# Whitening on neighbouring partitions, and a third depthwise tap on TensorE, in a four-layer hybrid kernel

## The chip, the cores and the metric

The kernel runs on one core of a Trainium2 chip. The metric is the device time of one execution in microseconds. Before the change three runs gave 7655.76, 7665.0 and 7673.1 us; their median is 7665.0 us.

## The reference

The input is x, 8 images of 56 x 56 pixels with 128 channels, float32. Four layers follow one another; the change touches the first two.

Layer 0 is a deformable convolution block. From each image it computes a depthwise 3x3 convolution, a batch norm and a gelu; a matrix product of that with `w_off` and `w_msk` gives, per pixel, 4 groups x 9 points x (two offsets and one mask logit). The masks go through a softmax over the 9 points. The image, projected by `w_in`, is then sampled bilinearly at each point plus its offset, weighted by the masks and summed; a projection, two layer norms and a small two-layer network follow. All offsets of the given data have a magnitude of at most 1.

Layer 1 is a decorrelating batch norm ("whitening"). The flat activation is seen as 64 rows. In outline:

```
x1_s  = every ninth element of each of the 64 rows
mean1 = mean of x1_s per row
cov   = x1_s x1_s^T / n  + 0.01 I          (64 x 64; x1_s as it is)
D     = cov^(-1/2), by five Newton-Schulz steps
y     = D (x1 - mean1)
```

The kernel takes its sample in two halves of a row, with the same stride. Layers 2 and 3 are token layers with attention and a mixture of experts; they take most of the time.

## The kernel before

**Layer 0.** `conv_layer` first prepares all images, then samples. Preparation is a loop over n from -1 to 8 that calls, in this order, `hidden(n-1)`, `image(n+1)`, `first_taps(n+1)`, `other_taps(n)`, on odd n `projection` of the pair (n-1, n), and `offsets(n-1)`. A scheduler of the framework decides the order on each engine from this program order, the data dependences and the buffers.

- `image` (L266, L271): loads an image (`xs`), transposes it on PE into PSUM (`p_x`) and copies it with seven ACT copies into `xp`, a padded image; two images share one `xp` tile, and there are two such tiles. Seven more ACT operations (L276) make strided copies `xT`, which SP's queue stores.
- `first_taps` (L315, L322): the first `NTE` of the nine taps of the depthwise convolution as products with diagonal matrices (`taps`), summed in PSUM (`p_dw`), seven pieces of 448 columns per image; ACT copies each piece to `acc`. A float32 product is two instruction records.
- `other_taps` (L327): the other taps on DVE, one multiply-add of 128x3136 each.
- `hidden` (L341): gelu on ACT, seven pieces.
- `projection` (L288, L295): `w_in` on the padded pair, with a bias addition on DVE, and stores into `strips` in device memory.
- `offsets` (L356 to L370): products `p_om`, seven additions on DVE into `om`, then a maximum and a negated minimum over all offsets of the image (L365, L366), which land in two columns of `far`, then `mask_softmax` (L430 to L435: maximum, subtraction, Exp on ACT, sum, reciprocal, multiplication), then a store of `om`.

After the loop the largest of all values in `far` is found (L393 to L398) and compared: `near` is 1 where it is at most 1. All engines load `near` and branch. `sample_near` relies on offsets of magnitude at most 1 and multiplies with small dense matrices; `sample_any` gathers with indirect DMAs. Before the loop, `zero` is written by two DMAs into the first and last two rows of `strips`, and sixteen small ones follow on the same queue, that of ACT.

**Layer 1.** `whiten_layer` holds the whole activation in SBUF as `x`, 128 partitions of 25,088 columns (12.85 MB). Partition h x 64 + b holds half h of row b, so each DMA (3,584 columns) reads 64 rows of one half into 64 partitions, fourteen in all on SP's queue. For each half: a reduction of the strided sample (`tot`, L900), 22 transposes of the sample (L912, 64x64 each out), 22 copies (L921) and 22 products of the piece with itself, summed in `cov` (L922). `p_mean` (L934) adds the sums of the two halves. Then come `a` (covariance plus 0.01 I), its norm, and five Newton-Schulz steps that alternate small PE products and DVE copies (L968 to L978). `both` (L983 to L986) is a 128x128 matrix with D in two diagonal blocks. For each of seven column ranges DVE subtracts the mean in place (L989), PE multiplies by `both` in seven pieces (`p_o`, L995), DVE and ACT copy alternately to `o`, and two DMAs of 64 partitions store it (L1003). The next layer reads y from device memory.

Of the kernel before, what the change touches and what calls it, by code (L numbers as in the profile page):

```python
# [17 lines left out]
NB, IH, IW, C = 8, 56, 56, 128  # L18
S = IH * IW
T = 112  # L20
NT = S // T
# [6 lines left out]
GP = GRP * NP  # L28
# [3 lines left out]
VW = IW + 4  # L32
PH, PX, NX = 7, 4, 14
SW = PX + 4
# [1 line left out]
R4 = 4 * C  # L36

NPX = 6
NTE = 2


WB, WCOLS, WSTEP, WITER, WEPS = 64, NB * S * C // 64, 9, 5, 0.01
WHALF = WCOLS // 2
# [84 lines left out]
def conv_layer(tc, k, x, w, z):  # L128

    nc = tc.nc  # L130
    n_batch = x.shape[0]
    with ExitStack() as ctx:
        cp = ctx.enter_context(tc.tile_pool(name="l0c", bufs=1))
# [30 lines left out]
        with tc.tile_pool(name="l0m", bufs=1) as mp:  # L164
            mean = mp.tile([128, 4], F32, name="mean")
# [13 lines left out]
            for b, name in ((q.b_out, "b_out"), (q.b2, "b_fc2")):  # L179
                row = row_bc(nc, mp, w[name], 128, name + "_row")  # L180
# [15 lines left out]
        gam = row_bc(nc, cp, w["gamma2"], T, "gam2r")  # L196
        nc.vector.tensor_tensor(q.sft2, q.sft2, gam, ALU.mult)

        far = cp.tile([T, 2 * n_batch], F32, name="far")
        near = cp.tile([1, 1], I32, name="near")  # L200
        with ExitStack() as pre:
            ip = pre.enter_context(tc.tile_pool(name="l0i", bufs=1))
            hp = pre.enter_context(tc.tile_pool(name="l0h", bufs=2))
            ps = pre.enter_context(tc.tile_pool(name="l0p", bufs=8, space=PSUM))
# [28 lines left out]
            nc.vector.tensor_tensor(bn_t, bn_t, bn_s, ALU.mult)  # L233
            nc.vector.tensor_tensor(bn_t, bn_t, bn_b, ALU.add)

            zero = ip.tile([NX * n_batch, 2 * SW * C], F32, name="zero")
            nc.gpsimd.memset(zero, 0.0)
            rows = q.strips.rearrange("n k y s c -> (n k) y (s c)")
            for y in (0, VW - 2):
                nc.scalar.dma_start(  # L240
                    rows[:, y : y + 2].rearrange("k y s -> k (y s)"), zero
                )
            for n in range(n_batch):
                for at in (q.strips[n, 0, :, :2], q.strips[n, NX - 1, :, SW - 2 :]):
                    nc.scalar.dma_start(
# [104 lines left out]
            def offsets(n, hT):  # L350

                om = hp.tile([T, NT, 3 * GP], F32, name="om")
                for r in range(PH):
                    p = ps.tile([T, GT, 3 * GP], F32, tag="m", name="p_om")
                    for i in range(GT):
                        nc.tensor.matmul(  # L356
                            p[:, i, :],
                            hT[:, r, i].rearrange("p a b -> p (a b)"),
                            w_om,
                            start=True,  # L360
                            stop=True,
                        )
                    nc.vector.tensor_tensor(om[:, r * GT : (r + 1) * GT, :], p, b_om, ALU.add)
                off = om[:, :, : 2 * GP]
                nc.vector.tensor_reduce(far[:, 2 * n : 2 * n + 1], off, AX.XY, ALU.max)  # L365
                nc.vector.tensor_reduce(  # L366
                    far[:, 2 * n + 1 : 2 * n + 2], off, AX.XY, ALU.min, negate=True
                )
                mask_softmax(nc, hp, om)
                nc.sync.dma_start(q.om[n], om)  # L370


# [51 lines left out]
def mask_softmax(nc, pool, om):  # L424

    n_t = om.shape[1]
    m = om[:, :, 2 * GP :].rearrange("p t (q g) -> p t g q", g=GRP)
    msum = pool.tile([T, n_t, GRP], F32, name="msum")
    mb = msum.unsqueeze(3).to_broadcast([T, n_t, GRP, NP])
    nc.vector.tensor_reduce(msum, m, AX.X, ALU.max)  # L430
    nc.vector.tensor_tensor(m, m, mb, ALU.subtract)
    nc.scalar.activation(om[:, :, 2 * GP :], om[:, :, 2 * GP :], AF.Exp)
# [433 lines left out]

def whiten_layer(tc, k, z, y):

    nc = tc.nc
    n_half = -(-WCOLS // WSTEP) // 2  # L870
    first = (0, -WHALF % WSTEP)
    n_tr = -(-n_half // 128)
    WC = 7 * 512
    zf = z.rearrange("h n w c -> (h n w c)").rearrange("(r s) -> r s", r=WB)
    yf = y.rearrange("h n w c -> (h n w c)").rearrange("(r s) -> r s", r=WB)
    with ExitStack() as ctx:
        bp = ctx.enter_context(tc.tile_pool(name="l1b", bufs=1))
        wp = ctx.enter_context(tc.tile_pool(name="l1w", bufs=3))
# [2 lines left out]
        ps1 = ctx.enter_context(tc.tile_pool(name="l1p1", bufs=1, space=PSUM))  # L881
        ps2 = ctx.enter_context(tc.tile_pool(name="l1p2", bufs=2, space=PSUM))


        x = bp.tile([2 * WB, WHALF], F32, name="x")
        for c in range(0, WHALF, WC):
            for h in range(2):
                nc.sync.dma_start(
                    x[h * WB : (h + 1) * WB, c : c + WC],
                    zf[:, h * WHALF + c : h * WHALF + c + WC],  # L890
                )


        smp = bp.tile([128, 2 * n_tr * WB], F32, name="smp")
        cov = ps1.tile([WB, WB], F32, name="cov")
        tot = bp.tile([2 * WB, 1], F32, name="tot")
        n_mm = 0
        for h in range(2):
            rows = slice(h * WB, (h + 1) * WB)
            nc.vector.tensor_reduce(  # L900
                tot[rows],
                x[rows, first[h] : first[h] + WSTEP * (n_half - 1) + 1 : WSTEP],
                AX.X,
                ALU.add,
            )
            for i0 in range(0, n_tr, 8):
                p = ps.tile([128, 8, WB], F32, tag="m", name="p_smp")
                m = min(8, n_tr - i0)
                for i in range(i0, i0 + m):
                    n = min(128, n_half - i * 128)  # L910
                    a = first[h] + i * 128 * WSTEP
                    nc.tensor.transpose(  # L912
                        p[:n, i - i0, :],
                        x[rows, a : a + WSTEP * (n - 1) + 1 : WSTEP],
                        k.ident[rows, rows],
                    )
                for i in range(i0, i0 + m):
                    n = min(128, n_half - i * 128)
                    at = (h * n_tr + i) * WB
                    s = smp[:n, at : at + WB]  # L920
                    nc.vector.tensor_copy(s, p[:n, i - i0, :])  # L921
                    nc.tensor.matmul(  # L922
                        cov, s, s, start=(n_mm == 0), stop=(n_mm == 2 * n_tr - 1)
                    )
                    n_mm += 1

        n_smp = float(2 * n_half)
        fold = bp.tile([2 * WB, 2, WB], F32, name="fold")
        for h in range(2):
            nc.vector.tensor_tensor(  # L930
                fold[:, h], k.ident[:, :WB], k.ident[:, WB:], ALU.add
            )
        p = ps.tile([2 * WB, 1], F32, tag="m", name="p_mean")
        nc.tensor.matmul(  # L934
            p, fold.rearrange("p a b -> p (a b)"), tot, start=True, stop=True
        )
        mean = bp.tile([2 * WB, 1], F32, name="mean")
        nc.vector.tensor_scalar(mean, p, 1.0 / n_smp, None, ALU.mult)
# [4 lines left out]
        nc.vector.scalar_tensor_tensor(a, cov, 1.0 / n_smp, ieps, ALU.mult, ALU.add)  # L943


        sq = bp.tile([WB, WB], F32, name="sq")
# [19 lines left out]
        for _ in range(WITER):  # L966
# [12 lines left out]
        dm = bp.tile([WB, WB], F32, name="dm")  # L979
        nc.vector.tensor_scalar(dm, zm, rinv, None, ALU.mult)  # L980
        both = bp.tile([2 * WB, 2 * WB], F32, name="both")
        nc.vector.memset(both, 0.0)
        nc.vector.tensor_copy(both[:WB, :WB], dm)  # L983
        p = ps2.tile([2 * WB, WB], F32, tag="ns", name="p_low")
        nc.tensor.matmul(p[WB:], k.ident[:WB, :WB], dm, start=True, stop=True)
        nc.vector.tensor_copy(both[WB:, WB:], p[WB:])  # L986

        for c in range(0, WHALF, WC):
            nc.vector.tensor_scalar(  # L989
                x[:, c : c + WC], x[:, c : c + WC], mean, None, ALU.subtract  # L990
            )
            o = wp.tile([2 * WB, WC], F32, name="o")
            for i in range(0, WC, 512):
                p = ps.tile([2 * WB, 512], F32, tag="m", name="p_o")
                nc.tensor.matmul(  # L995
                    p, both, x[:, c + i : c + i + 512], start=True, stop=True
                )
# [4 lines left out]
            for h in range(2):  # L1002
                nc.sync.dma_start(  # L1003
                    yf[:, h * WHALF + c : h * WHALF + c + WC],
                    o[h * WB : (h + 1) * WB],
                )

# [1378 lines left out]
```

## Time and profile before

| | |
|---|---|
| median of three runs | 7665.0 us |
| profiled execution | 7657.94 us |
| its span | 7656.2 us |
| mean granted TensorE clock | 0.908 |
| layer 0: last multiplication of the preparation ends | 433.2 us |
| layer 0: sampling starts on DVE | 443.3 us |
| layer 1: first load of `x` issued | 1437.8 us |
| layer 1: last load of `x` lands | 1496.05 us |
| layer 1: `both` ready | 1531.9 us |
| layer 1: last stores of y issued | 1577.3 us |
| layer 2: first load of y issued | 1589.05 us |

Times inside the profile are counted from the start of the span. The profile's parts are: busy time of each engine (PE is TensorE, PEld its weight loads, DVE VectorE, ACT ScalarE, POOL GpSimd, SP the sync engine whose queue issues DMAs); the span in 40 slices; groups of instructions by line with the mean time of one and the idle time ahead of them; waits; and windows, which give each engine's busy time in a stretch. "L327" is a line of the kernel before. In a group, "out<-in" are the program's tile names, followed by the shapes and by the number of instructions.

### The profile page before, as it was taken

The page shows a single profiled execution, that of the slowest core. Times are in us where ns is not written, and L with a number is a line of the kernel's source. Part 1 is how long each engine was busy: PE and PEld are TensorE (multiplying, and loading weights), DVE is VectorE, ACT ScalarE, POOL GpSimd, SP SyncE. Part 2 cuts the span into 40 slices and gives each one's busy share as a digit, 9 for nine tenths or more (in the row PEclk, how much of TensorE's full clock was granted, in tenths as well). Part 3 has the DMA queues.
Part 4 walks back from the last instruction along what each step waited for, and adds up shares of the span by engine and source line. Part 5 has one row for each costly group of instructions (what it writes and reads, how often), then busy time and mean ns, then how long its engine had stood idle before and what let it go on. Part 6 is the DMA issues. An engine that isn't in the chain of part 4 may idle for free. (4 is left out here: it accounts for less than half of the span.)

```text
span 7656.2 us, 158331 instructions
## 1 busy us (share of the span) xinstructions
PE 6459.4 (84%) x59947; PEld 2867.8 (37%) x59947; DVE 5281.9 (69%) x9840; ACT 4163.3 (54%) x6499; POOL 2939.2 (38%) x2555
## 2 busy tenths in 40 slices
PE   6659999565899999999999999999999999556764
PEld 4446666333233333333333323323323323235542
DVE  7975564356677777777777777777777777356761
ACT  4424444122566666666666666666666666146750
POOL 0001111022344444444444444444444444333763
PEclk9768899776999999999999999999999999789877
DMA  5453343376787877778777778878778777544544
GB/s 156 135 121 78 85 97 65 83 227 215 191 207 191 197 188 192 197 190 195 197 191 192 197 187 197 198 188 196 195 191 197 190 185 181 198 111 113 137 134 142
DMA packets 737846, 1287.45 MB, mean 168 GB/s; under 512 B 119235, under 2 KB 504645, under 8 KB 730053
## 3 DMA queue, kind: packets, MB, share of 16 engines
q1 hardware_dynamic: 727092, 1260.77, 65.5%
q0 software_dynamic: 6144, 12.60, 0.5%
q8 instruction: 486, 7.96, 0.4%
q10 hardware_dynamic: 3824, 3.68, 0.2%
q14 instruction: 300, 2.45, 0.1%
HBM read 286.04 MB, written 197.81 MB: 63 GB/s over the span
## 5 line engine op out<-in xcount | busy, mean ns | idle before, releaser
L1260 ACT ACTIVATE e<-p_s 128x768 f32<-128x768 f32 (+2 forms) x3712 | 2887.8, 830 | 1588.2 <-PE p_s L1252 1320.1
L1298 POOL COPY x<-sq 32x1152 f32<-32x1152 f32 x1792 | 2062.2, 1151 | 2017.6 <-PE p_s L1252 1241.2
L1271 DVE STREAM_TRANSPOSE sq<-e 128x768 f32<-128x768 f32 x2688 | 2434.3, 950 | 516.0 <-ACT e L1260 258.9
L1252 PE MATMUL p_s<-q,kT 32*128 32x384 f32 (+2 forms) x14848 | 1892.8, 548 | 37.8 <-ACT e L1260 21.9
L1305 PE MATMUL av<-e,va 128*32 128x384 f32 (+2 forms) x14848 | 1646.5, 515 | 13.3 <-DVE acc L1328 8.3
L1305 PE MATMUL avx<-x,va 128*32 128x384 f32 x10752 | 1134.3, 494 | 62.2 <-issue 38.9
L1252 PEld LDWEIGHTS p_s<-q,kT 32*128 32x128 f32 (+1 forms) x14848 | 649.3, 181 | 1266.1 <-issue 837.7
L1305 PEld LDWEIGHTS av<-e,va 128*32 128x32 f32 (+1 forms) x14848 | 294.0, 108 | 1030.7 <-issue 936.9
L1305 PEld LDWEIGHTS avx<-x,va 128*32 128x32 f32 x10752 | 351.5, 111 | 642.4 <-issue 601.9
L609 POOL TENSOR_TENSOR rs<-rs,mhalf 112x4 f32<-112x4 f32 x112 | 116.1, 1036 | 789.8 <-DVE rs L608 789.8
L1324 DVE TENSOR_TENSOR acc<-acc,avx 128x384 f32<-128x384 f32 x336 | 183.8, 547 | 232.5 <-PE avx L1305 229.5
L121 PE MATMUL p_tr<-ident,xn 112*128 112x112 f32 x672 | 133.5, 338 | 188.6 <-DVE xn L112 141.8
L1141 POOL TENSOR_TENSOR rs<-rs,mhalf 112x4 f32<-112x4 f32 (+2 forms) x136 | 167.9, 1235 | 249.6 <-DVE ntop L1986 123.5
L525 ACT COPY wT<-p_w 88x448 f32<-88x448 f32 x152 | 137.8, 921 | 193.1 <-PE p_w L523 193.1
L2034 ACT ACTIVATE xn<-t,ms,rs 112x128 f32<-112x128 f32 x448 | 185.2, 487 | 76.2 <-DVE ms L2027 76.2
L327 DVE SCALAR_TENSOR_TENSOR acc<-xp,dw,acc 128x3136 f32<-128x3136 f32 x56 | 193.9, 3471 | 29.8 <-ACT acc L322 29.7
L637 PE MATMUL p_f<-x1T,w 128*128 128x448 f32 x448 | 209.4, 593 | 4.4 <-DVE x1T L632 2.8
L121 PEld LDWEIGHTS p_tr<-ident,xn 112*128 112x128 f32 x672 | 97.5, 167 | 282.0 <-issue 186.6
L523 PE MATMUL p_w<-ident,wide 112*88 112x112 f32 x896 | 146.6, 303 | 58.6 <-DMA px<-strips 34.1
L1394 POOL TENSOR_TENSOR rs_b<-rs_b,mhalf 128x3 f32<-128x3 f32 (+1 forms) x72 | 58.5, 815 | 356.5 <-DVE rs_b L1393 347.0
L621 DVE TENSOR_TENSOR y<-y,p_rs 128x448 f32<-128x448 f32 x112 | 69.3, 619 | 182.2 <-PE p_rs L614 182.2
L122 ACT COPY xT<-p_tr 128x448 f32<-128x448 f32 x112 | 59.6, 532 | 229.2 <-PE p_tr L121 204.5
(363 smaller groups left out, 7816.5 us busy)
## 6 DMA issues: line engine op xcount, KB each, us to landing
x<-sq SPq DMA_DIRECT2D x5376, 144.0 KB
w<-in_L_ffn_weight_dram SPq DMA_DIRECT2D x64, 1024.0 KB
px<-strips SPq DMA_DIRECT2D x64, 616.0 KB
va_d<-va SPq DMA_DIRECT2D x16, 1600.0 KB
xT_d<-xT SPq DMA_DIRECT2D x112, 224.0 KB
xT<-xT_d SPq DMA_DIRECT2D x112, 224.0 KB
kT_d<-kT SPq DMA_DIRECT2D x16, 1568.0 KB
t<-t_a SPq DMA_DIRECT2D x16, 1568.0 KB
```

The lines of the kernel that those rows point to most:

```text
L121: nc.tensor.transpose(p[:, i, :], src[:, i, :], k.ident[:T, :T])
L327: nc.vector.scalar_tensor_tensor(acc, xp[:, j // 3 : j // 3 + IH, j % 3 : j % 3 + IW], dw[:, j : j + 1], acc, ALU.mult, ALU.add,)
L523: nc.tensor.transpose(p[:, g], around[:, :, g], k.ident[:T, :T])
L637: nc.tensor.matmul(p, q.w1[:, f * 128 : (f + 1) * 128], x1T, start=True, stop=True)
L1141: nc.gpsimd.tensor_tensor(rs, rs, k.mhalf[:m, :n], ALU.pow)
L1252: nc.tensor.matmul(ss[j // 2][:m, j % 2, :width], kT[rows, 128 * i : 128 * i + m], q[rows, :width], start=True, stop=True,)
L1260: nc.scalar.activation(e[:m, 2 * j : 2 * j + 2, :width], ss[j][:m, :, :width], AF.Exp)
L1271: nc.vector.transpose(sq[:, :, i, j : j + 2].rearrange("p s j c -> p j s c"), exps[u, b, a, i][:, j : j + 2, :QB].rearrange("p j (s c) -> ...
L1298: nc.gpsimd.tensor_copy(*moves.pop(0))
L1305: nc.tensor.matmul(out, keys[u, b][1][:m, i, j, :], e[j], start=start, stop=stop)
L1324: nc.vector.tensor_tensor(to, to, in_order(av), ALU.add)
L2034: nc.scalar.activation(out[:, i], x[:, i], AF.Identity, bias=ms[:, i : i + 1], scale=rs[:, i : i + 1])
```

## The change

The number of taps on TensorE goes from two to three, and VectorE does six instead of seven. The two reductions over the offsets are replaced by four ACT operations after the softmax: Relu of (offset - 1) and of (-offset - 1), on each half of the tiles, whose sums over the free dimension (`accum_out`) land in four columns of `far`; `near` is 1 where no sum is above 0. `zero` is half as long, and four DMAs write what two wrote. In `whiten_layer` partition 2b + h holds half h of row b, so loads and stores are one DMA of 128 partitions each, seven and seven. A transpose covers both halves at once (128x128 out) and the copies pick every second column; the sample has a 65th column of ones, so the covariance product gives the sums as well. The matrices `at[:, h]` spread 64 rows over every second partition and are used for the mean and to lay out `both`.

```diff
-NTE = 2
+NTE = 3
...
-        far = cp.tile([T, 2 * n_batch], F32, name="far")
+        far = cp.tile([T, 4 * n_batch], F32, name="far")
...
+            minus = ip.tile([T, 1], F32, name="minus")
+            nc.vector.memset(minus, -1.0)
...
-            zero = ip.tile([NX * n_batch, 2 * SW * C], F32, name="zero")
+            zero = ip.tile([NX * n_batch, SW * C], F32, name="zero")
...
-            for y in (0, VW - 2):
-                nc.scalar.dma_start(
-                    rows[:, y : y + 2].rearrange("k y s -> k (y s)"), zero
-                )
+            for y in (0, 1, VW - 2, VW - 1):
+                nc.scalar.dma_start(rows[:, y], zero)
...
-                nc.vector.tensor_reduce(far[:, 2 * n : 2 * n + 1], off, AX.XY, ALU.max)
-                nc.vector.tensor_reduce(
-                    far[:, 2 * n + 1 : 2 * n + 2], off, AX.XY, ALU.min, negate=True
-                )
                 mask_softmax(nc, hp, om)
+
+                over = ip.tile([T, NT // 2, 2 * GP], F32, name="over")
+                for a in range(4):
+                    nc.scalar.activation(
+                        over,
+                        off[:, a // 2 * NT // 2 : (a // 2 + 1) * NT // 2],
+                        AF.Relu,
+                        bias=minus,
+                        scale=1.0 - 2.0 * (a % 2),
+                        accum_out=far[:, 4 * n + a : 4 * n + a + 1],
+                    )
...
-            nc.vector.tensor_scalar(near, one, 1.0, None, ALU.is_le)
+            nc.vector.tensor_scalar(near, one, 0.0, None, ALU.is_le)
...
-    zf = z.rearrange("h n w c -> (h n w c)").rearrange("(r s) -> r s", r=WB)
+    zf = z.rearrange("h n w c -> (h n w c)").rearrange("(r s) -> r s", r=2 * WB)
...
         for c in range(0, WHALF, WC):
+            nc.sync.dma_start(x[:, c : c + WC], zf[:, c : c + WC])
+        at = bp.tile([WB, 2, 2 * WB], F32, name="at")
+        nc.vector.memset(at, 0.0)
+        for h in range(2):
+            nc.vector.tensor_copy(at[:, h, h::2], k.ident[:WB, :WB])
+        smp = bp.tile([128, 2, n_tr, WB + 1], F32, name="smp")
+        nc.gpsimd.memset(smp, 1.0)
+        cov = ps1.tile([WB, WB + 1], F32, name="cov")
...
+                for i, n in sizes:
                     a = first[h] + i * 128 * WSTEP
                     nc.tensor.transpose(
+                        p[:n, i - i0, :], x[:, a : a + WSTEP * (n - 1) + 1 : WSTEP], k.ident
                     )
+                whole = [i for i, n in sizes if n == 128]
+                if whole:
+                    nc.vector.tensor_copy(
+                        smp[:, h, i0 : i0 + len(whole), :WB], p[:, : len(whole), h::2]
+                    )
...
+                    s = smp[:n, h, i]
                     nc.tensor.matmul(
+                        cov, s[:, :WB], s, start=(n_mm == 0), stop=(n_mm == 2 * n_tr - 1)
                     )
...
+        row = bp.tile([WB, 1], F32, name="mean_row")
+        nc.vector.tensor_scalar(row, cov[:, WB:], 1.0 / n_smp, None, ALU.mult)
+        p = ps.tile([2 * WB, 1], F32, tag="m", name="p_mean")
         for h in range(2):
+            nc.tensor.matmul(p, at[:, h], row, start=(h == 0), stop=(h == 1))
...
+        for h in range(2):
+            nc.vector.tensor_scalar(dm[:, h, h::2], zm, rinv, None, ALU.mult)
+        p = ps2.tile([2 * WB, 2 * WB], F32, tag="ns", name="p_both")
+        for h in range(2):
+            nc.tensor.matmul(p, at[:, h], dm[:, h], start=(h == 0), stop=(h == 1))
         both = bp.tile([2 * WB, 2 * WB], F32, name="both")
+        nc.vector.tensor_copy(both, p)
...
+            nc.sync.dma_start(yf[:, c : c + WC], o)
```

More of the change, by code (lines that the diff above doesn't have):

```diff
@@ L873, in whiten_layer @@
     WC = 7 * 512
-    zf = z.rearrange("h n w c -> (h n w c)").rearrange("(r s) -> r s", r=WB)
-    yf = y.rearrange("h n w c -> (h n w c)").rearrange("(r s) -> r s", r=WB)
+    zf = z.rearrange("h n w c -> (h n w c)").rearrange("(r s) -> r s", r=2 * WB)
+    yf = y.rearrange("h n w c -> (h n w c)").rearrange("(r s) -> r s", r=2 * WB)
     with ExitStack() as ctx:
@@ L886, in whiten_layer @@
         for c in range(0, WHALF, WC):
-            for h in range(2):
[L888 to L910, printed above, removed]
+            nc.sync.dma_start(x[:, c : c + WC], zf[:, c : c + WC])
@@ new lines, in whiten_layer @@
+        at = bp.tile([WB, 2, 2 * WB], F32, name="at")
[5 more added lines that the diff above has]
+        cov = ps1.tile([WB, WB + 1], F32, name="cov")
+        n_mm = 0
+        for i0 in range(0, n_tr, 4):
+            sizes = [(i, min(128, n_half - i * 128)) for i in range(i0, min(i0 + 4, n_tr))]
+            for h in range(2):
+                p = ps.tile([128, 4, 2 * WB], F32, tag="m", name="p_smp")
+                for i, n in sizes:
@@ L911, in whiten_layer @@
                     a = first[h] + i * 128 * WSTEP
                     nc.tensor.transpose(
-                        p[:n, i - i0, :],
-                        x[rows, a : a + WSTEP * (n - 1) + 1 : WSTEP],
-                        k.ident[rows, rows],
-                    )
[L917 to L921, printed above, removed]
+                        p[:n, i - i0, :], x[:, a : a + WSTEP * (n - 1) + 1 : WSTEP], k.ident
+                    )
@@ L922, in whiten_layer @@
+                whole = [i for i, n in sizes if n == 128]
[3 more added lines that the diff above has]
+                    )
+                for i, n in sizes:
+                    if n < 128:
+                        nc.vector.tensor_copy(smp[:n, h, i, :WB], p[:n, i - i0, h::2])
+                    s = smp[:n, h, i]
                     nc.tensor.matmul(
-                        cov, s, s, start=(n_mm == 0), stop=(n_mm == 2 * n_tr - 1)
+                        cov, s[:, :WB], s, start=(n_mm == 0), stop=(n_mm == 2 * n_tr - 1)
@@ L927, in whiten_layer @@
         n_smp = float(2 * n_half)
-        fold = bp.tile([2 * WB, 2, WB], F32, name="fold")
+        row = bp.tile([WB, 1], F32, name="mean_row")
+        nc.vector.tensor_scalar(row, cov[:, WB:], 1.0 / n_smp, None, ALU.mult)
+        p = ps.tile([2 * WB, 1], F32, tag="m", name="p_mean")
         for h in range(2):
[L930 to L936, printed above, removed]
+            nc.tensor.matmul(p, at[:, h], row, start=(h == 0), stop=(h == 1))
         mean = bp.tile([2 * WB, 1], F32, name="mean")
-        nc.vector.tensor_scalar(mean, p, 1.0 / n_smp, None, ALU.mult)
+        nc.vector.tensor_copy(mean, p)
         a = bp.tile([WB, WB], F32, name="a")
@@ L942, in whiten_layer @@
         nc.vector.tensor_scalar(ieps, k.ident[:WB, :WB], WEPS, None, ALU.mult)
-        nc.vector.scalar_tensor_tensor(a, cov, 1.0 / n_smp, ieps, ALU.mult, ALU.add)
+        nc.vector.scalar_tensor_tensor(
+            a, cov[:, :WB], 1.0 / n_smp, ieps, ALU.mult, ALU.add
+        )
         sq = bp.tile([WB, WB], F32, name="sq")
@@ L978, in whiten_layer @@
             nc.vector.tensor_copy(zm, p)
-        dm = bp.tile([WB, WB], F32, name="dm")
-        nc.vector.tensor_scalar(dm, zm, rinv, None, ALU.mult)
-        both = bp.tile([2 * WB, 2 * WB], F32, name="both")
[L982 to L986, printed above, removed]
+        dm = bp.tile([WB, 2, 2 * WB], F32, name="dm")
+        nc.gpsimd.memset(dm, 0.0)
+        for h in range(2):
[3 more added lines that the diff above has]
+            nc.tensor.matmul(p, at[:, h], dm[:, h], start=(h == 0), stop=(h == 1))
+        both = bp.tile([2 * WB, 2 * WB], F32, name="both")
+        nc.vector.tensor_copy(both, p)
         for c in range(0, WHALF, WC):
@@ L1001, in whiten_layer @@
                     nc.scalar.copy(o[:, i : i + 512], p)
[L1002 to L1006, printed above, removed]
+            nc.sync.dma_start(yf[:, c : c + WC], o)
 def load_tokens(nc, dst, src):
```

## The prediction

> **What bounds the kernel now.** I read the page first (engine shares and the 40 slices of 191.4 us), then stage windows, groups and waits of the two stages that the change touches. The program is one serial chain of layers, so a stage is worth what ends last in it.
>
> ```profile
> PE 6459.4 (84%) x59947; PEld 2867.8 (37%) x59947; DVE 5281.9 (69%) x9840; ACT 4163.3 (54%) x6499; POOL 2939.2 (38%) x2555
> DVE  7975564356677777777777777777777777356761
> GB/s 156 135 121 78 85 97 65 83 227 215 191 207 191 197 188 192 197 190 195 197 191 192 197 187 197 198 188 196 195 191 197 190 185 181 198 111 113 137 134 142
> ```
>
> PE's 84% is earned in the attention layers, which keep their instruction order; what counts here are the first two and a bit DVE slices (layer 0 preparation, to 433 us) and the eighth (whitening, 1436 to 1601). The windows of these stages (columns: stretch, length, busy us of PE, PEld, DVE, ACT, POOL with counts, PE clock, DMA share, GB/s):
>
> ```profile
> core 0: us, PE busy (x) PEld busy (x) DVE busy (x) ACT busy (x) POOL busy (x), PEclk, DMA share, GB/s
> 121.00:213.00 92.00, 66.43 (x336) 51.02 (x335) 89.00 (x57) 47.59 (x62) 0.00 (x0) 0.83 0.56 155
> 213.00:305.00 92.00, 66.54 (x337) 51.13 (x336) 89.00 (x57) 47.47 (x62) 0.00 (x0) 0.83 0.52 149
> 397.00:434.00 37.00, 10.99 (x110) 10.55 (x108) 33.91 (x32) 2.08 (x2) 0.00 (x0) 0.71 0.63 176
> 1436.00:1496.00 60.00, 9.89 (x68) 8.13 (x68) 5.17 (x38) 0.00 (x0) 0.00 (x0) 0.50 0.96 210
> 1496.00:1532.00 36.00, 13.58 (x101) 10.88 (x101) 30.52 (x46) 1.65 (x3) 0.00 (x0) 0.59 0.04 9
> 6660.00:6675.00 15.00, 10.18 (x136) 4.10 (x136) 0.66 (x3) 2.37 (x4) 0.00 (x0) 1.00 1.05 389
> ```
>
> Each pair of images costs 92.2 us (offset additions begin at 121.09, 213.31, 305.49 and 397.46), and DVE is busy 89 of 92: it sets preparation, with PE next at 66. Whitening waits 60 us for loads at 210 GB/s with every engine idle, then 36 us with DVE busy 30.5. The last row, outside the change, is a stretch of 128-row expert loads: same chip, 389 GB/s. The groups of preparation (busy, mean ns, idle before):
>
> ```profile
> L327 DVE SCALAR_TENSOR_TENSOR acc<-xp,dw,acc 128x3136 f32<-128x3136 f32 x56 | 193.9, 3471 | 29.8 <-ACT acc L322 29.7
> L315 PE MATMUL p_dw<-xp,taps 128*128 128x448 f32 x205 | 85.9, 573 | 9.4 <-DVE om L363 7.4 <-ACT xp L271 2.0
> L365 DVE TENSOR_REDUCE far<-om 112x1 f32<-112x2016 f32 x8 | 18.0, 2247 | 0.0
> L366 DVE TENSOR_REDUCE far<-om 112x1 f32<-112x2016 f32 x8 | 17.9, 2238 | 0.0
> L432 ACT ACTIVATE om<-om 112x1008 f32<-112x1008 f32 x8 | 8.4, 1044 | 39.6 <-DVE om L431 39.6
> ```
>
> and of whitening, with one line of its waits:
>
> ```profile
> PE p_smp L912 <- DMA x<-z: 56.9, 7, 16.6
> L900 DVE TENSOR_REDUCE tot<-x 64x1 f32<-64x2788 f32 x2 | 10.2, 5118 | 2.8 <-DMA x<-z 2.8
> L989 DVE TENSOR_SCALAR x<-x,mean 128x3584 f32<-128x3584 f32 x7 | 14.5, 2072 | 0.0
> L995 PE MATMUL p_o<-x,both 128*128 128x512 f32 x98 | 44.2, 614 | 0.3 <-DVE both L986 0.3
> ```
>
> **What the Trainium skill says.** "SBUF — State Buffer", section "Door 1: The DMA port swizzle", says rows 0 to 63 reach 8 of 16 DMA ports: 196 GB/s at 1 MiB, about 218 at best, against 328 and 436 for 128 rows. The trace agrees: 64-row loads run at 215 to 227 GB/s, 128-row ones at 389, above the page's 328 for their size. "DMA: Bandwidth & Descriptors", section "Rules for kernel authors", says that two transfers to the two halves serialise; here a pair of halves (1.835 MB) takes 8.3 us, 220 GB/s, as one alone would. "ScalarE: Activation LUTs", section "Table sets: the hidden batching unit", has relu in every table set: the four Relus should cost no table load, and the changed order shows none added; the trace before has no Relu here. "TensorE: Matmul & The Clock Gate", "Part 1: The HAM clock gate", has PE at half speed until it has been busy some microseconds; before, p_dw records follow each other every 0.75 us at first, 0.376 later.
>
> **Preparation, DVE.** Removed per image: one tap (L327, issued every 3.40 us) and two reductions (L365, L366, every 2.16). 8 × 3.40 = 27.2 and 16 × 2.16 = 34.6: 61.8 us of DVE in 433.
>
> **Preparation, PE and ACT.** Third tap: 14 more p_dw records per image at 0.376 = 5.3 us. A pair on PE: offsets 11.2, image transposes 5.7, p_dw 21.4, projection 22.7 = 61.0 before, 71.6 after. ACT per image: about 24 us, plus four Relus of 112x1008. No such row exists; the nearest is the Exp of L432, 1.04 us, plus an accumulator read as on L1993, 0.19: 4 × 1.23 = 4.9. Bounds: 4 × 0.61 (the L1993 Exp of 448) to 4 × 1.6 if read and write do not overlap. Both engines are below DVE's 92 − 15.4 = 77 us a pair, so they hide on average; but not everywhere, because in the changed order each image's Relus stand on ACT ahead of or between the seven copies that fill the next image (xp from p_x), behind which wait that image's p_dw on PE and DVE's next tap.
>
> Step by step. The first image's taps begin on DVE at 53.7; with 5.3 more on PE at 58.3 to 59. In the first pair PE now sets the end: p_dw(0) to 58.3, p_x(1) 61.1, p_dw(1) 76.7, p_x(2) 79.5, p_dw(2) 95.4, projection to 118.1, offsets 123.7; the additions of image 0 end at 126.0, where they ended at 126.34, so nothing is gained, except that one tap of image 2 is already done. From there three pairs: about 82 (gelu 6.7 and Relus 4.9 before the copies, then p_dw 15.8, projection 22.7 and offsets 5.6 in a row on PE), 79.5 and 77.5 (DVE's own sum), together 239 against 92.7 + 2 × 92.2 = 277.1. The tail from the additions of image 6 to the last multiplication was 29.7 with four reductions (8.6); after, 21.6. So preparation ends at 126.0 + 239 + 21.6 = 386.6, not 433.2: **46.6 us**. Bounds: 61.8 less 1 to 2 if DVE alone counts, 30 if PE or ACT sets every pair at about 86.
>
> The zero strips (four DMAs for two, ahead of sixteen on ACT's queue, which held ACT's first copy until 39.9) may shift the start by ±3; taken as 0. If gone wrong, everything behind ACT's first copy shifts by it. The near test needs no more time: its Relus end before DVE's last steps.
>
> **Whitening, loads.** 12.85 MB now take 58.3 us (first issued 1437.8, last landing 1496.05). Seven 128-row DMAs at 385 GB/s: 33.4 + 2 = 35.4 us, **−22.9**. At the page's 328: 41, −17. At 220: 0.
>
> **Whitening, last landing to `both`.** Before: 35.8 us (to 1531.88), of which the two sums cost 10.2 in a row; mean at +12.0, `a` at +14.2. After: the last eight 128x128 transposes (0.27 each at the cold clock) with their copies and covariance products, then one scaling, two small products and a copy: mean at about +7.4. From `a` to `both` was 21.6 us, 14.5 of it DVE's seven subtractions that share DVE with the Newton–Schulz steps; these stay, with a doubled last copy and product (+0.6 to 1.5). `both` at about +31.3: **−4.5**, bounds −2 and −7.
>
> **Whitening, stores.** From the first p_o to the issue of the next layer's load: 57.1 us, of which PE 44.2; the last stores are issued at 1577.3, the load at 1589.05. Seven full stores keep up with PE (33.4 at 385) and two of eight weight loads stand ahead of the last store: the 11.7 us drain becomes 7 to 9, **−4**, bounds 0 and −6.
>
> Sum: 46.6 + 22.9 + 4.5 + 4 = 78.0. Against the profiled 7657.94 (span 7656.2) that is 7580; the runs' median is 7665.0, so 7587. Everything later keeps its order and shifts as a block.
>
> **Rivals.** (a) *Preparation becomes PE- or ACT-bound throughout*: for it, Relus wait in front of the copies that feed PE, and PE rises to 72 of 77; against it, each engine alone has slack. Gain 25 to 35 there: total 62, 7603. (b) *Loads stay at 220*: for it, the DMA share was already 0.96; against it, the same share moved 389 GB/s with 128 rows. The first −22.9 and the −4 vanish: total 51, 7614. (c) *DVE's count comes out whole*: 61 in preparation, total 92, 7573. It needs PE not to set the first pair. (d) *Slower: the test fails.* If one of 112 × 32 sums comes out above zero, the other branch runs: 28 tiles × 36 gathers × 8 images = 8064 indirect issues on POOL at 0.94 us (L1727, L1807) = 7.6 ms for the 1.0 ms of the near branch: about 14,250. Against it: x − 1 and −x − 1 keep their sign exactly in f32, so it hangs only on Relu giving exactly zero below zero.
>
> **How the numbers follow.** Forecast 0.50 (its own range 7575 to 7598), (a) 0.18, (b) 0.08, (c) 0.19, (d) 0.02; 0.03 for mixtures that reach about no change. Runs of one kernel spread ±9. Range 7562 to 7615. About 0.2% (15 us) is what a measurement can tell: faster 0.95, same 0.02, slower 0.03.
>
> **What would show it.** Pair period 77 to 82 with DVE busy nearly all of it (PE above 90% in the first pair); last multiplication near 387. Relu near 1.2 us with its read. x loads landing 35 us after their issue at 370 GB/s or more, mean 7 us later, `both` at +31. Wrong if pairs stay at 86 or more with DVE waiting for p_dw copies, or if loads stay at 220.

## The result

The changed kernel takes 7564.6 us (median; 7555.6 to 7579.74) beside 7660.38 us of the kernel before in the same set: ratio 0.9878, 95% interval 0.9852 to 0.9904, so 74 to 113 us faster and 96 us in the middle. Two later measurements beside other kernels gave 7580.29 (ratio 0.9898, 0.9883 to 0.9914; 82 us) and 7571.17 (ratio 0.9882, 0.9867 to 0.9897; 89 us). The forecast was 78 us, 7587.

First the page of the changed kernel: engine shares, and DVE in 40 slices, now of 189.2 us.

```profile
PE 6499.5 (86%) x60063; PEld 2893.4 (38%) x60063; DVE 5210.3 (69%) x9787; ACT 4198.0 (55%) x6563; POOL 2941.4 (39%) x2557
DVE  7866664366677777777777777777777777356761
```

The shares hardly tell anything: DVE lost 72 busy us (5281.9 to 5210.3) and kept its 69%. The stages do. A pair of images is counted from the first addition of offsets (L363) of an even image to that of the next even image. The windows of the changed kernel lie roughly on the three pairs of preparation, then on the loads of whitening and on the chain from covariance to `both`:

```profile
core 0: us, PE busy (x) PEld busy (x) DVE busy (x) ACT busy (x) POOL busy (x), PEclk, DMA share, GB/s
120.00:202.00 82.00, 73.54 (x358) 56.26 (x357) 76.30 (x50) 53.41 (x76) 0.00 (x0) 0.92 0.63 170
202.00:282.00 80.00, 74.88 (x372) 56.98 (x371) 71.44 (x50) 51.68 (x74) 0.00 (x0) 0.98 0.60 163
282.00:360.00 78.00, 53.67 (x297) 44.97 (x296) 73.89 (x51) 48.20 (x63) 0.00 (x0) 0.80 0.53 152
1393.00:1428.00 35.00, 16.06 (x104) 12.77 (x105) 5.03 (x13) 0.00 (x0) 1.68 (x2) 0.61 0.88 368
1428.00:1455.00 27.00, 10.71 (x71) 7.76 (x69) 19.78 (x39) 1.65 (x3) 0.00 (x0) 0.61 0.00 1
```

In the first two of these windows PE (74 and 75 us) and DVE (76 and 71) are now level, where it was 66 and 89 before; in the third PE has 54 and DVE 74. The loads move 368 GB/s instead of 210. The groups of preparation (busy, mean ns, idle before):

```profile
L327 DVE SCALAR_TENSOR_TENSOR acc<-xp,dw,acc 128x3136 f32<-128x3136 f32 x48 | 166.5, 3470 | 37.6 <-ACT acc L322 37.3
L315 PE MATMUL p_dw<-xp,taps 128*128 128x448 f32 x324 | 127.3, 552 | 10.0 <-ACT xp L271 10.0
L369 ACT ACTIVATE over<-om,minus 112x1008 f32<-112x1008 f32 x32 | 36.1, 1129 | 29.0 <-DVE om L363 28.8
L369 ACT ACTIVATION_READ_ACCUMULATOR over<-om,minus 112x1 f32 x32 | 6.2, 195 | 0.0
```

Eight multiply-adds and the sixteen reductions are gone; a Relu with its read takes 1.13 + 0.195 = 1.32 us, where the forecast had 1.23. There are seven table loads for gelu and seven for Exp in this stretch, as before: the Relus add none, as the Trainium skill ("ScalarE: Activation LUTs", "Table sets: the hidden batching unit") says. PE's waits for the loads of whitening fell from 56.9 us to 26.5:

```profile
PE p_smp L913 <- DMA x<-z: 26.5, 7, 15.8
```

Where the time went is seen when the span is cut at five events, each read from the trace's starts: last multiplication of the preparation done (the last store of `om` is issued), first DVE step of sampling, first load of `x`, first load of y by layer 2, end of the span.

| us | before | changed | gain |
|---|---|---|---|
| start to last multiplication | 433.3 | 388.6 | 44.7 |
| to the first step of sampling | 10.0 | 16.0 | -6.0 |
| sampling, to the first load of `x` | 994.5 | 989.2 | 5.3 |
| whitening, to the first load of y | 151.3 | 114.2 | 37.1 |
| all layers behind, to the end | 6067.1 | 6058.5 | 8.6 |
| span | 7656.2 | 7566.5 | 89.7 |

The lines that the change touches account for 44.7 - 6.0 + 37.1 = 75.8 us. The other 13.9 lie in stages whose instructions are unchanged.

### The profile page after: what moved, and what is told of

Its sections match the earlier page's. It is cut to its first block, busy times and chain, and to the rows that moved or that the text cites. A ratio compares the mean times of both kernels' runs of the same rounds, so it can differ in the third digit from the quotient of the medians.

```text
span 7566.5 us, 158564 instructions
## 1 busy us (share of the span) xinstructions
PE 6499.5 (86%) x60063; PEld 2893.4 (38%) x60063; DVE 5210.3 (69%) x9787; ACT 4198.0 (55%) x6563; POOL 2941.4 (39%) x2557
## 5 line engine op out<-in xcount | busy, mean ns | idle before, releaser
L1304 PE MATMUL av<-e,va 128*32 128x384 f32 (+2 forms) x14848 | 1644.2, 515 | 13.5 <-DVE acc L1327 8.5
L327 DVE SCALAR_TENSOR_TENSOR acc<-xp,dw,acc 128x3136 f32<-128x3136 f32 x48 | 166.5, 3470 | 37.6 <-ACT acc L322 37.3
```

The lines of the kernel that those rows point to most:

```text
L327: nc.vector.scalar_tensor_tensor(acc, xp[:, j // 3 : j // 3 + IH, j % 3 : j % 3 + IW], dw[:, j : j + 1], acc, ALU.mult, ALU.add,)
L1304: nc.tensor.matmul(out, keys[u, b][1][:m, i, j, :], e[j], start=start, stop=stop)
```

## The experiments

**The parts alone.** Three kernels take one part each, or the two parts of preparation together. The third tap and the Relus need SBUF that the shorter `zero` tile frees, so these kernels have it too.

The tap alone (e1_tap):

```diff
-NTE = 2
+NTE = 3
...
-            for y in (0, VW - 2):
+            for y in (0, 1, VW - 2, VW - 1):
```

The Relus alone (e2_relu):

```diff
-                nc.vector.tensor_reduce(far[:, 2 * n : 2 * n + 1], off, AX.XY, ALU.max)
...
+                for a in range(4):
+                    nc.scalar.activation(
+                        over,
...
-            nc.vector.tensor_scalar(near, one, 1.0, None, ALU.is_le)
+            nc.vector.tensor_scalar(near, one, 0.0, None, ALU.is_le)
```

e4_prep has both of these, and e3_whiten has every line of the change within `whiten_layer` and no other:

```diff
-    zf = z.rearrange("h n w c -> (h n w c)").rearrange("(r s) -> r s", r=WB)
+    zf = z.rearrange("h n w c -> (h n w c)").rearrange("(r s) -> r s", r=2 * WB)
...
```

> The kernel before with the third tap on TensorE alone (and the zero strips in four DMAs, which make the room for it). Theory (TensorE sets the first pair, DVE the later ones): three pairs gain 6.8 us each, the first pair nothing or loses 2 to 3, the tail nothing: the last multiplication of the preparation ends at 413 to 417 instead of 433.2, the program is 16 to 20 us faster. Rival (DVE's busy time alone counts): 8 x 3.40 = 27 us, last multiplication near 406.

> The kernel before with the two reductions replaced by four Relus on ACT (and the zero strips in four DMAs). Theory (DVE sets every pair, ACT hides its 5.3 us per image): 8.6 us less in each of three pairs and in the tail, minus 1.5 at the start: last multiplication near 400 to 402, the program 31 to 34 us faster. Rival (the Relus hold the copies that feed TensorE): 20 us or less, with DVE waiting for copies of p_dw.

> The kernel before with the changed whitening alone. Theory: what the trace of the changed kernel shows from the first load of x to the first load of y, 37 us, is the whole of this part, wherever it stands: 33 to 40 us faster. Rival (part of the 90 us of the pair of profiles lies in the attention layer, 11 us, and comes with whitening): 45 to 50 us.

> The kernel before with both changes of the preparation and none of whitening. Theory: as in the changed kernel, the last multiplication ends near 388.6, 44 us earlier, and the program is 42 to 46 us faster; less than the sum of the two parts alone, since with both TensorE sets the first two pairs. Rival (parts add up): the sum of e1 and e2.

Measured, with the stages cut as above (the kernel before in this set: 7662.62 us; ratios are to it):

| | median us | ratio, 95% interval | last multiplication | to sampling | sampling | whitening | behind |
|---|---|---|---|---|---|---|---|
| e1_tap | 7635.96 | 0.9969 (0.9959 to 0.9980) | 412.0 | 10.0 | 990.2 | 151.2 | 6058.9 |
| e2_relu | 7633.65 | 0.9967 (0.9955 to 0.9980) | 399.9 | 18.5 | 992.3 | 151.1 | 6060.8 |
| e3_whiten | 7627.16 | 0.9955 (0.9942 to 0.9967) | 434.6 | 10.5 | 997.4 | 114.9 | 6075.6 |
| e4_prep | 7626.18 | 0.9952 (0.9940 to 0.9965) | 388.1 | 15.6 | 999.7 | 152.3 | 6073.8 |

The tap alone gains 21.3 us up to the last multiplication, a little above the theory's 16 to 20, and short of the 27 that DVE's busy time would give. The Relus alone gain 33.4, as the theory had it. Together they gain 45.2, not the sum 54.7. Most of what is missing lies in the first pair: it lasts 84.8 us with the tap, 84.2 with the Relus and still 83.4 with both, where the second lasts 85.4, 83.8 and 78.7. Whitening is worth 36.4 us alone (151.3 to 114.9) and 37.1 with the rest of the change.

The medians of the whole programs tell less. They lie 26.7, 29.0, 35.5 and 36.4 us below the kernel before, each with an interval of 8 to 10 us to either side. By its median the tap would suit the rival, and e2 and e4 fall short of their forecasts (31 to 34 and 42 to 46 us), but each forecast reaches into its interval. The readings above rest on the stages.

Two columns had not been expected. "To sampling" is 10 us with the tap alone and 15 to 19 wherever the Relus are. And "behind", where no line of these kernels differs, runs from 6058.5 to 6075.6, the kernel before in the middle: the 8.6 us that the pair of profiles shows there come and go with the execution. Sampling varies likewise, from 989 to 1000 here.

**How wide a transfer is.** The changed kernel, but each load of `x` in two DMAs of 64 partitions:

```diff
-            nc.sync.dma_start(x[:, c : c + WC], zf[:, c : c + WC])
+            for h in range(2):
+                half = slice(h * WB, (h + 1) * WB)
+                nc.sync.dma_start(x[half, c : c + WC], zf[half, c : c + WC])
```

> The changed kernel with each load of x issued as two DMAs, partitions 0 to 63 and 64 to 127, so the same bytes to the same places in fourteen transfers of 64 partitions. Theory (64 partitions reach half of the ports): the last landing comes 58 us after the first issue again instead of 34, and the program is 22 to 25 us slower than the changed kernel. Rival (it was the layout in device memory, neighbouring half rows, or the size of a transfer that mattered): 34 to 40 us, the same time as the changed kernel.

It takes 7607.22 us (ratio to before 0.9931, 0.9918 to 0.9945; 27 us more than the changed kernel in the same set, where 22 to 25 had been forecast). A wait of this kernel, and the window from its first load to PE's last wait for one:

```profile
PE p_smp L915 <- DMA x<-z: 55.4, 7, 21.0
```

```profile
1395.00:1459.00 64.00, 17.68 (x101) 14.07 (x102) 4.19 (x13) 0.00 (x0) 0.93 (x2) 0.50 0.95 201
```

The same bytes to the same places take 64 us at 201 GB/s instead of 34. So neither the layout in device memory nor anything PE does sets the rate. The size of a transfer does not explain it either: these halves have 0.9 MB, and the expert loads in the prediction, 1 MB each on 128 rows, moved 389 GB/s. What is left is the partitions of a single transfer, as the Trainium skill has it ("SBUF — State Buffer", "Door 1: The DMA port swizzle"). The DMA share was 0.95 here and 0.88 at 368 GB/s: that share shows that engines are occupied, not how fast they move data.

**What stands in the chain of whitening, and at the start.** Two edits in one kernel, in different stages:

```diff
-            nc.vector.tensor_scalar(
-                x[:, c : c + WC], x[:, c : c + WC], mean, None, ALU.subtract
-            )
+        p = ps.tile([2 * WB, 1], F32, tag="m", name="p_shift")
+        nc.tensor.matmul(p, both, mean, start=True, stop=True)
+        nc.vector.tensor_scalar(shift, p, -1.0, None, ALU.mult)
...
-                    nc.vector.tensor_copy(o[:, i : i + 512], p)
+                    nc.vector.tensor_scalar(o[:, i : i + 512], p, shift, None, ALU.add)
...
-                    nc.scalar.copy(o[:, i : i + 512], p)
+                    nc.scalar.activation(o[:, i : i + 512], p, AF.Identity, bias=shift)
...
-                nc.scalar.dma_start(rows[:, y], zero)
+                nc.gpsimd.dma_start(rows[:, y], zero)
```

(The sixteen small zero DMAs move to GpSimd's queue as well.)

> The changed kernel with the mean taken out after the product (one small product of the whitening matrix with the mean, added as a bias in the copies of p_o) in place of the seven subtractions, and with the zero strips on GpSimd's queue instead of ACT's. Theory: the seven subtractions (14.5 us on DVE) stand in the Newton-Schulz chain, from mean to the first p_o 23 us shrink to 12 to 15; the first copy of the first image, held on ACT until 41.4 by the zero DMAs, comes at about 33, the first pair of the preparation 4 to 5 us earlier: 12 to 16 us faster than the changed kernel. Rival (the Newton-Schulz chain alone takes the 23 us, and other work holds the first pair): within 3 us of the changed kernel.

It takes 7560.09 us (ratio to before 0.9867, 0.9852 to 0.9882), 20 us less than the changed kernel in its set. In the timeline (start, duration) `mean` and `both` of this kernel come at

```profile
1438.73 0.16 DVE L937 COPY mean<-p_mean 128x1 f32<-128x1 f32 x1 [0.56 <-PE p_mean L935]
1452.27 0.29 DVE L989 COPY both<-p_both 128x128 f32<-128x128 f32 x1 [1.15 <-PE p_both L987]
```

which is 13.5 us apart; in the changed kernel `mean` is copied at 1432.02 and `both` at 1454.86, 22.8 us. So 9.3 of the subtractions' 14.5 us were not hidden. Up to the first load of y whitening takes 106.6 us instead of 114.2. At the start, ACT's first copy of the changed kernel and then of this one:

```profile
41.43 3.15 ACT L271 COPY xp<-p_x 128x448 f32<-128x448 f32 x7 [20.86 <-DMA strips<-zero]
```

```profile
30.39 0.53 ACT L271 COPY xp<-p_x 128x448 f32<-128x448 f32 x1 [12.02 <-PE p_x L266]
```

The zero DMAs on ACT's queue did hold the first image (in the kernel before until 39.94, with four instead of two until 41.43); without them the copies follow PE, and the last multiplication ends at 380.8, 7.6 us earlier than the changed kernel in this set (388.4). The two stages together gain 15 us, within the forecast of 12 to 16; the 20 us of the medians are more than the forecast and than what these stages show.

**Where the Relus stand.**

```diff
+            def excess(n, om):
+                off = om[:, :, : 2 * GP]
+                over = ip.tile([T, NT // 2, 2 * GP], F32, name="over")
+                for a in range(4):
...
                     accs[n + 1] = first_taps(place(n + 1))
+                if late is not None:
+                    excess(*late)
+                    late = None
...
-                    offsets(n - 1, hT)
+                    late = offsets(n - 1, hT)
+            excess(*late)
```

> The changed kernel with the four Relus of an image issued after the next image's first taps, so that on ACT they stand behind the copies that feed TensorE. Theory (they hold the copies and with them TensorE in the first pairs): the pair of 83.5 us shrinks to 78 to 80, the last multiplication ends 3 to 5 us earlier. Rival (TensorE's own work sets that pair): 83 us, no change within 1 us.

7567.82 us (ratio 0.9881, 0.9866 to 0.9896), 12 us below the changed kernel in its set, but the intervals overlap. The trace decides: additions of the offsets begin at 120.93, 198.32, 276.63 and 353.34, so the pairs last 77.4, 78.3 and 76.7 us instead of 83.6, 78.8 and 77.9, and the last multiplication ends at 380.4, 8.0 us earlier. The windows of the first two pairs:

```profile
121.00:198.00 77.00, 73.12 (x362) 56.81 (x362) 73.22 (x50) 51.72 (x74) 0.00 (x0) 0.96 0.64 173
198.00:276.00 78.00, 73.62 (x363) 56.27 (x363) 73.82 (x51) 53.40 (x76) 0.00 (x0) 0.96 0.61 167
```

PE does the same 73 us of work in 77 instead of 83.6. The theory held, and the gain was larger than the 3 to 5 us expected.

**One tap more.**
```diff
-NTE = 3
+NTE = 4
```

> The changed kernel with four taps on TensorE instead of three. Theory (TensorE is the next bound right behind DVE): a pair costs TensorE 71.6 + 10.6 = 82 us and DVE 70, so all pairs last 82 us or more, the last multiplication ends at 397 or later instead of 388.5, and the program is 8 to 20 us slower than the changed kernel. Rival (DVE still sets the pairs): 6.8 us less per pair, the last multiplication near 370.

```profile
121.00:203.00 82.00, 82.00 (x398) 61.13 (x399) 68.31 (x50) 49.55 (x72) 0.00 (x0) 1.00 0.64 170
203.00:285.00 82.00, 82.00 (x399) 61.13 (x399) 68.71 (x49) 53.91 (x77) 0.00 (x0) 1.00 0.58 163
```

In these two stretches PE never idles, and DVE is idle for nearly 14 us of 82: with four taps TensorE is the bound here. The pairs themselves begin at 140.76, 219.58, 303.82 and 369.52, so they last 78.8, 84.2 and 65.7 us, and not 82 or more each, as the theory had it. The last multiplication ends at 395.6, 7 us later than with three taps. The whole program does not follow: 7582.16 us (ratio 0.9906, 0.9890 to 0.9923), an interval that overlaps the changed kernel's, and in its profile sampling took 974.5 us, 15 us less than in any other profile here. This profile is of the fastest of its four runs (7565.67 us; the others took 7581 to 7584). Why is not settled.

**The three edits together, and the stores at the end of preparation.**

> The changed kernel with all three edits of the two kernels before it in this study: Relus behind the copies, mean taken out after the product, zero strips on GpSimd's queue. Theory (the gains lie in different places and add): the last multiplication ends near 372, whitening takes 107 us from the first load of x to the first load of y, and the median is 7545 to 7560. Rival (the stores at the end of the preparation, which already held the sampling back for 12 us in the changed kernel, become the bound): sampling starts near 395 as with one edit alone, median 7565.

7558.00 us (ratio 0.9875, 0.9858 to 0.9891). By the trace the gains add where they were expected: last multiplication at 370.5, sampling from 386.7 and not from 395 as the rival had it, first load of y at 1486.5, against 1508.0 to 1516.5 in the three profiles of the changed kernel. What is left of it at the end, 97 us below the kernel before against 82 to 96, is within the intervals. So the medians do not show that it beats the changed kernel; the trace up to layer 2 does.

It still waits 16.2 us from the last multiplication to sampling. The timelines of the kernel before and then of the changed one around this gap (start, duration, engine):

```profile
431.23 1.96 DVE L435 TENSOR_TENSOR om<-om,msum 112x1008 f32<-112x1008 f32 x1
433.25 0.34 SPq L370 DMA_DIRECT2D om_d<-om  x1
439.57 0.80 SPq L480 DMA_DIRECT2D om<-om_d  x2
```

```profile
386.61 1.96 DVE L442 TENSOR_TENSOR om<-om,msum 112x1008 f32<-112x1008 f32 x1
388.63 0.34 SPq L377 DMA_DIRECT2D om_d<-om  x1
400.66 0.80 SPq L487 DMA_DIRECT2D om<-om_d  x2
```

From the last store of `om` to the first load of sampling it was 6.3 us, and now it is 12.0. The DMA view of the changed kernel from 395 to 401 us says what runs in that time:

```profile
DMA  1010030000100100100100100100100100000000
DMA packets 15, 0.13 MB, mean 22 GB/s; under 512 B 4, under 2 KB 4, under 8 KB 4
```

Fifteen packets, one at a time, with a mean share of 0.06, which is one engine of sixteen: one DMA engine finishes alone what the others finished by 396. In the kernel before, the last store of `om` (433 to 439.5 us) had them all at once:

```profile
DMA  0000009939909698987949859959513300100000
DMA packets 128, 1.35 MB, mean 208 GB/s; under 512 B 16, under 2 KB 16, under 8 KB 16
```

The waits of SP ahead of the first load of sampling name what was late, in the kernel before (first line) and in the changed one:

```profile
SPq L480 <- DMA om_d<-om: 4.7, 1, 4.7
SPq L487 <- DMA om_d<-om: 6.7, 2, 3.6
SPq L487 <- DMA strips<-pj: 3.7, 2, 3.1
```

Before, the last store of `om` was all that was missing. Now stores of `strips` are still on their way as well. The test of the offsets is not what sampling waits for: `near` was ready at 383.7, before the last multiplication ended (388.6). One more kernel asked whether that engine's queue is the cause:

```diff
-                nc.sync.dma_start(q.om[n], om)
+                nc.gpsimd.dma_start(q.om[n], om)
```

> The kernel with all three edits, and the stores of om on GpSimd's queue instead of SP's, so that they need not stand behind the stores of strips. Theory (the last om store lands late because on one DMA engine it is queued behind strips stores of the same queue): from the last multiplication to the first DVE step of sampling 10 to 12 us instead of 16, the program up to 5 us faster than with the three edits. Rival (sampling waits for the strips stores themselves, or that engine is busy whatever the queue): 15 to 17 us, no gain.

15.3 us instead of 16.2, and 7559.28 us (ratio 0.9867, 0.9849 to 0.9885): the theory of the queue fell. The last packets come singly in this kernel too. The trace records when each part of a transfer has landed, and these times tell more (us; the last store of `om` lands in sixteen parts):

| | last `strips` store landed | last `om` store issued | its fifteenth part landed | its last part landed |
|---|---|---|---|---|
| before | 425.5 | 433.3 | 438.8 | 439.4 |
| e1_tap | 402.5 | 412.0 | 417.6 | 418.1 |
| e2_relu | 407.7 | 400.0 | 409.4 | 414.3 |
| changed | 393.8 | 388.6 | 395.9 | 400.6 |
| e13_queue | 375.5 | 373.3 | 382.1 | 383.2 |

In the three profiles without the Relus (before, e1 and e3) the stores of `strips` had landed 8 to 10 us before the last store of `om` was issued, and that store landed 6.1 us after its issue. In all eleven with the Relus they landed 2 to 8 us after that issue, and the store took 10 to 14 us. So the gap comes with a tail of DVE that has become too short to cover the stores of `strips`. The other queue did not change this overlap. All this is read from the order in time in fourteen profiles; no kernel was run that moves or spreads the stores of `strips` alone, and why one engine is so far behind the others with them stays open.

**The changed kernel again.**

> The changed kernel once more, beside the others of this set. Theory (the stages' sum of the traces is the effect, 76 to 81 us, and what the first measurement showed beyond it lies in how long the attention layer happens to take): median 76 to 85 us below the kernel before. Rival (the attention layer gains too): 90 to 98 us.

> The changed kernel beside it on the same chip. Theory: 76 to 85 us below the kernel before, and 20 to 28 us above the kernel with the three edits, which is the sum of the traces up to the first load of y. Rival: under 10 us apart, since the layers behind use the difference up.

82 and 89 us below the kernel before; the second is above the forecast of 76 to 85. Their stages up to the first load of y sum to 74.4 and 72.5 us less than the profile of the kernel before has, and 81.0 in the first profile; the layers behind took 6061.9 and 6068.7. Against the kernel with the three edits, by first loads of y, the distance is 28 and 30 us; by the medians against the kernel with the queue edit besides, which was timed beside it, 12. So the theory (20 to 28) holds roughly for the stages and not for the medians, and the rival (under 10) was nearly right there.

## Why the prediction was right, and where it was not

The forecast of 78 us was right in sign and place, somewhat low against the measured 82 to 96, and close to what the touched stages show (76). That it is so close to 76 is in part luck. Preparation gave 1.9 us less than its 46.6 and whitening 5.7 more than its 31.4, and 6.0 were lost in a wait that the forecast did not have; these nearly cancel. Step by step:

| step of the prediction | forecast | changed kernel |
|---|---|---|
| DVE's first tap | 58.3 to 59 | 61.73 |
| additions of image 0 end | 126.0 | 128.5 |
| the three pairs | 82, 79.5, 77.5 | 83.6, 78.8, 77.9 |
| tail | 21.6 | 21.7 |
| last multiplication ends | 386.6 | 388.6 |
| wait from there to sampling | as before (10) | 16.0 |
| first load of `x` to last landing | 35.4 | 33.7 |
| last landing to `both` | 31.3 | 27.7 |
| first p_o to the first load of y | 53.1 | 52.8 |

*Preparation.* The working in pairs was right to within 1.6 us at every pair, and a count of DVE's busy time (61.8 us) would have been wrong by 17: rival (c) fell, and e1, e2 and e4 agree, since the parts do not add. Two of its sums are not quite what the prediction shows: the terms given for the pair of 82 add to 55.7, so that the rest of that pair is not shown, and 29.7 less 8.6 is 21.1, not 21.6. The reason given for the long first pair, Relus ahead of the copies that feed PE, is shown by e10: moved behind them, they leave 77.4 us. So what rival (a) feared came true in one pair of three, and not throughout.

*The start.* The zero strips were taken as 0 within ±3 us: the first copy came 1.5 us later, and about eight p_dw records followed each other at 0.75 us, where five had before, another 1.1 us. The first tap was about 3 us late, and the last multiplication 2.0.

*The step that failed* is "everything later ... shifts as a block". The Relus shortened DVE's tail from 29.7 to 21.7 us, and the stores that the tail used to cover became what sampling waits for: 6 us. In the changed kernel the last of `strips` landed 5.1 us after the last store of `om` was issued, where it had landed 7.8 us before. The prediction asked what is late next only for the stores of y, and not for those of `om` and `strips`.

*Whitening.* Loads were sized from the expert loads (389 GB/s) and came at 12.85 MB in 33.7 us, 381 GB/s. Rival (b) fell with that, and e5 shows what it hung on. The 1496.05 that the table of the kernel before and the prediction take for the last landing is the end of PE's last wait, for the thirteenth of fourteen transfers. By the trace the last one landed at 1499.59, 61.8 us after the first issue, so that the whole ran at 208 GB/s and not 220. Its part of the sample was not needed yet, since DVE was still adding up the other half until 1501.3, and so the chain of this stage can be cut at 1496.05 all the same.

"Last landing to `both`" was mis-sized by 3.6 us: mean came 4.5 us after the last landing and not 7.4. Eight transposes did follow the last landing, as the prediction had it, but the last of them began 2.6 us after it, and copies and covariance products ran beside them. How the 7.4 were put together the prediction does not show. The drain of the stores was 6.5 us, just under the 7 to 9 of the forecast.

*Rival (d)* did not come: the near branch was taken, as its loads in the timeline show.

*What lies beyond the sum.* The attention and expert layers, with the same instructions, took 6058 to 6076 us in these profiles, and sampling 974 to 1001. The prediction used ±9 for the spread of runs. The last 6 to 20 us of the measured gain cannot be assigned to the change from these runs.

## What to carry to other kernels

When work moves off the bound engine, add up the next engine's stretch between two waits, and not its mean load: TensorE had slack on the mean and still held up the first pair, because ACT's new work stood in front of the copies that fed it. Load with all 128 partitions in one transfer, and choose the layout for it. And when a tail becomes shorter, ask which stores it used to cover.

## What the runs showed of the hardware

- From first issue to last landing, transfers of 64 partitions moved 202 and 208 GB/s (e5, before) and those of 128 partitions 381, for the same bytes. In the windows of these loads the DMA share was 0.95, 0.96 and 0.88: the slower transfers showed the higher share.
- A store is done when the slowest of its parts is. In the changed kernel fifteen of the sixteen parts of the last `om` store had landed by 395.9 us and the last at 400.6, and the load that needs it was issued at 400.66. From 395 to 401 us 0.13 MB moved, one packet at a time, 22 GB/s.
- DMAs issued from ACT's queue hold ACT's compute. In the changed kernel the last of the zero strips was issued at 40.92 us and ACT's first copy came at 41.43, though the transposes that feed it had begun at 31.52. With the zero strips on GpSimd's queue the copy came at 30.39, 1.1 us after its first transpose.
- The layers behind, in which no line differs, took 6058 to 6076 us from profile to profile, a spread of 17 us and of the size of most single effects measured here; the stages' own times tell apart what the medians can't.
